# First batches' inverse root on ScalarE, and another order of the first loads, in a resampler-attention and top-1-MoE kernel

## The chip, the cores and the metric

The kernel runs on one core of one Trainium2 chip. The metric is the device time of one execution in microseconds; lower is better. A core has TensorE (PE, with its weight loads as PEld), VectorE (DVE), ScalarE (ACT), GpSimd (POOL) and SyncE (SP). SP, ACT and POOL also issue DMAs, and each of these engines works through its own instructions in the order in which the program gives them.

## The reference, cut to what matters

Sixteen batches of 128 rows of 256 numbers pass through cross-attention and then through a mixture of experts. Everything that the change touches lies in the attention's input side:

```python
def layer_norm(x, w, b):
    mu = jnp.mean(x, axis=-1, keepdims=True)
    var = jnp.var(x, axis=-1, keepdims=True)
    return (x - mu) * jax.lax.rsqrt(var + EPS) * w + b
...
x = layer_norm(x, ln1_w, ln1_b)                        # x here: the context rows
lat = layer_norm(latents, ln2_w, ln2_b)                # latents: _layernorm of the residual rows
lat = lat * (1.0 + scale[:, None, :]) + shift[:, None, :]
q = jnp.einsum('bld,ed->ble', lat, Wq)
kv_in = jnp.concatenate((x, lat), axis=-2)
kv = jnp.einsum('bld,ed->ble', kv_in, Wkv)
k, v = jnp.split(kv, 2, axis=-1)
...
w = jax.nn.softmax(logits.astype(jnp.float32), axis=-1)
out = jnp.einsum('bhqk,bhkd->bhqd', w, v)
```

After the output product the result is added to the residual, normed again, routed to one of eight experts per row and also sent through a shared expert. There are 16 heads of 64; all numbers are float32.

## The kernel before, in words

The batches go in pairs. For a pair `g`, `inputs(g)` or `norms(...)` computes mean and variance of each row, an inverse root of the variance, the normed rows, their transpose, and a scaled and shifted copy `kvT` (columns: 128 context rows and 128 latent rows of a batch). `k_unit(b, j)`, `v_unit(b, j)` and `q_unit(g, j)` are pieces of the products with the weights `wk`, `wv`, `wq`: each fills one PSUM buffer of the pool `ps_m` (three buffers, taken in turn), and ScalarE copies it out (lines 454, 472, 438). `step(u, ...)` handles half the heads of one batch: `logits`, row maxima on DVE, exponents on ScalarE, the division by the sums on POOL, a transpose of the weights through DRAM, and the product with `v`. Between these parts it calls the pieces in the list `units`, in the order of the list, so that PE has work. After the last step come the shared expert, the routing and the experts.

The order on every engine is the order of the calls in the Python code (line 76, `manual_schedule`, for all five engines). Only the data waits are added, and one wait of another sort: each DMA from SP or ACT counts its landing on one of eight counters, and a DMA that takes a counter for the second time waits, on its issuing engine, until the earlier DMA of that counter has landed.

The first pair is handled apart, by `first_inputs(0)` and `first_inputs(1)`, one batch each:

- Lines 97 to 100: DVE clears a tile, and PE runs `WARM` = 9 products on it, so that it isn't idle while the first data travel.
- Lines 281 to 294: the first loads. SP issues `xres` (residual rows of batch 0), `wk` (1024 KB), `xres` of batch 1, the router, and two rows of zeros for DRAM tables; ACT issues `ctx` (context rows of batch 0), `vec` (20 KB: condition vectors and the norms' weights), `ctx` of batch 1, `wv`, `wq` and `wo` (1024 KB each). Of these `wq` waits for the landing of the first `ctx`, `wo` for that of `vec`, and the row of zeros of line 294 for that of `wk`.
- `modulation()` (lines 300 to 310) makes `mod_w` and `mod_b` from `vec` on POOL.
- `first_inputs(i)` (lines 387 to 420): `bn_stats` and `bn_aggr` of the two row tiles (395, 396), the variances (398, 399), then `newton` (line 120): a start value from the bits of the number and three iterations, twelve DVE instructions on 128x2 numbers (lines 124 to 135). `normed` (line 140) makes `fz`, one instruction of 128x256 for each of the two tiles. PE transposes the four 128x128 blocks (410). DVE copies chunk 0 of both tiles into `kvT` (416), ScalarE copies chunk 1 of both (418).
- The calls then are: `modulation`, `first_inputs(0)`, four `k_unit(0, j)`, `first_inputs(1)`, loads of pair 1, `v_unit(0, 0)`, the norms of pair 1, four `q_unit(0, j)`, and `step(0)` with units `k1[0], k1[1], second_inputs, k1[2], k1[3], q[0], q[1]`. `second_inputs` transposes both chunks of pair 1 (359, 360) and loads pair 2.

Outside the first pair, the inverse roots keep `newton` in both kernels.

## Time and profile before

| what | value |
|---|---|
| median of 3 runs | 748.63 us (748.04 to 748.77) |
| the profiled execution's own time | 748.45 us |
| its span, first to last instruction | 746.6 us |
| TensorE clock granted, mean over the span | 0.999 |
| PE busy | 736.0 us (99%) |
| DVE, ACT, POOL busy | 385.8, 259.1, 314.4 us |
| first product with `wk` starts | 9.32 us from the span's start |
| DMA traffic in 0 to 30 us | 5.56 MB |

"Busy" is the time in which an engine has at least one instruction of the program under way. In the timeline a row gives start, duration, engine, source line, operation, what it writes and reads, and in brackets how long the engine had been idle before and what ended that. ACTq and SPq are the sequencers of ACT and SP, where DMAs are issued and where an issue waits. A product of float32 numbers shows as two records, so the nine warm-up products are 18 matmuls.

### The profile page before, as it was taken

Reading aid. Unit: us, or ns where it says so; the run is one execution under the profiler, and the core shown is the slowest. Engines: PE = TensorE matmul, PEld = TensorE weight load, DVE = VectorE, ACT = ScalarE, POOL = GpSimd, SP = SyncE. Lnnn points to the kernel's source line nnn. Section 1 sums busy time; section 2 is a strip of 40 time slices with the busy share of each in tenths; the row PEclk is TensorE's granted clock in tenths of the full one; section 3 lists DMA queues with packets and bytes.
Section 4 is the critical chain, followed back from the end, with each engine's and each line's share of the span. In section 5 each row is a group of like instructions: output and inputs, shape, how many; then the busy total and the mean of one; then the engine's idle time right before and its main releaser. Section 6 shows DMA issues by size and latency. Waiting matters only on the chain.

```text
span 746.6 us, 11560 instructions
## 1 busy us (share of the span) xinstructions
PE 736.0 (99%) x4096; PEld 572.5 (77%) x4096; DVE 385.8 (52%) x949; ACT 259.1 (35%) x787; POOL 314.4 (42%) x366
## 2 busy tenths in 40 slices
PE   8999999999999999999999999999999999999997
PEld 6857768777677677687686788688888877778886
DVE  5566558558647656665656437634643333333321
ACT  2444534444354354344444554611311011111111
POOL 1363554464355445534643654440104334444220
PEclk9999999999999999999999999999999999999999
DMA  8075735844953953864664634651991345645301
GB/s 297 17 250 195 204 128 179 235 165 154 270 170 127 264 200 129 218 223 143 193 197 137 203 124 165 208 183 56 306 322 55 83 110 154 173 138 162 97 27 46
DMA packets 140773, 125.20 MB, mean 168 GB/s; under 512 B 62484, under 2 KB 124631, under 8 KB 140708
## 3 DMA queue, kind: packets, MB, share of 16 engines
q1 hardware_dynamic: 134356, 108.49, 46.8%
q0 software_dynamic: 4336, 12.46, 5.4%
q10 hardware_dynamic: 2016, 3.43, 1.3%
q8 instruction: 35, 0.57, 0.3%
q14 instruction: 30, 0.25, 0.1%
HBM read 75.49 MB, written 49.02 MB: 167 GB/s over the span
## 4 chain that ended last, share of the span: by engine, by line
PE 93%; DVE 4%; ACT 2%; issue 0%; DMA 0%; ACTq 0%
PE pk L446 15%; PE pv L465 14%; PE u_w L1249 11%; PE S L498 8%; PE O L563 8%; PE p L162 8%; PE pw L579 7%; PE pq L431 7%; PE yr L1279 7%; PE ys L192 5%; ACT pe L517 1%; PE pr L634 1%; PE pr L162 1%; PE ys L245 1%; PE slots L983 0%
## 5 line engine op out<-in xcount | busy, mean ns | idle before, releaser
L530 POOL TENSOR_SCALAR pe<-pe,rs 128x256 f32<-128x256 f32 x256 | 232.5, 926 | 243.7 <-DVE rs L527 243.7
L517 ACT ACTIVATE pe<-S,nmx 128x256 f32<-128x256 f32 x256 | 118.7, 489 | 132.0 <-DVE nmx L510 132.0
L465 PE MATMUL pv<-wv,kvT 128*128 128x512 f32 x256 | 116.5, 599 | 0.2 <-ACT kT L454 0.2
L446 PE MATMUL pk<-kvT,wk 128*128 128x256 f32 x512 | 115.2, 383 | 1.3 <-ACT kT L454 0.7
L446 PEld LDWEIGHTS pk<-kvT,wk 128*128 128x128 f32 x512 | 95.8, 190 | 19.4 <-DVE px L539 2.0
L539 DVE STREAM_TRANSPOSE px<-pe 128x512 f32<-128x512 f32 x128 | 81.4, 682 | 32.0 <-POOL pe L530 32.0
L465 PEld LDWEIGHTS pv<-wv,kvT 128*128 128x128 f32 x256 | 47.2, 190 | 53.2 <-issue 50.6
L1249 PE MATMUL u_w<-xT,w 128*128 128x256 f32 (+2 forms) x352 | 85.6, 399 | 0.3
L1249 PEld LDWEIGHTS u_w<-xT,w 128*128 128x128 f32 x352 | 66.0, 190 | 18.8 <-DVE mid_w L1258 3.3
L510 DVE TENSOR_REDUCE nmx<-S 128x4 f32<-128x1024 f32 x64 | 75.1, 1213 | 9.7 <-PE S L498 9.5
L162 PE MATMUL p<-hT,ws 128*128 128x256 f32 x320 | 73.8, 382 | 0.2 <-DVE mid L178 0.2
L162 PEld LDWEIGHTS p<-hT,ws 128*128 128x128 f32 x320 | 59.9, 190 | 10.0 <-issue 1.3
L563 PEld LDWEIGHTS O<-pT,v 128*64 128x64 f32 x1024 | 55.2, 137 | 14.7 <-issue 12.9
L498 PE MATMUL S<-kT,qT 64*128 64x256 f32 x512 | 63.9, 389 | 0.0
L563 PE MATMUL O<-pT,v 128*64 128x128 f32 x1024 | 63.0, 276 | 0.0
L472 ACT COPY v<-pv 128x512 f32<-128x512 f32 x64 | 38.2, 599 | 63.1 <-PE pv L465 63.1
L527 DVE RECIPROCAL rs<-sums 128x4 f32<-128x4 f32 x64 | 11.4, 177 | 93.4 <-ACT pe L517 93.4
L579 PEld LDWEIGHTS pw<-wo,oT 128*128 128x128 f32 x256 | 48.6, 190 | 12.2 <-issue 3.1
L579 PE MATMUL pw<-wo,oT 128*128 128x256 f32 x256 | 57.9, 379 | 0.0
L431 PE MATMUL pq<-kvT,wq 128*128 128x256 f32 x256 | 57.7, 379 | 0.0
L1257 ACT ACTIVATE rsl_w<-u_w 128x256 f32<-128x256 f32 (+2 forms) x40 | 16.0, 400 | 118.8 <-PE u_w L1249 118.8
L517 ACT ACTIVATION_READ_ACCUMULATOR pe<-S,nmx 128x1 f32 x256 | 56.6, 221 | 0.0
(212 smaller groups left out, 748.5 us busy)
## 6 DMA issues: line engine op xcount, KB each, us to landing
p_blocks<-px SPq DMA_DIRECT2D x64, 512.0 KB, 3.2
pT<-p_blocks SPq DMA_DIRECT2D x64, 512.0 KB, 4.2
w<-in_w_dram SPq DMA_DIRECT2D x8, 704.0 KB, 6.3
wds<-in_w_dram SPq DMA_DIRECT2D x8, 640.0 KB, 8.3
w<-in_w_dram SPq DMA_DIRECT2D x8, 640.0 KB, 5.6
t_blocks<-tx SPq DMA_DIRECT2D x12, 256.0 KB, 2.4
kvT<-t_blocks SPq DMA_DIRECT2D x12, 256.0 KB, 6.2
h_rows<-h SPq DMA_DIRECT2D x8, 256.0 KB, 3.1
```

Source lines behind the costliest of these rows:

```text
L162: nc.tensor.matmul(ps, lhsT=shared["w13"][:, c, ds(col, P)], rhs=hT[:, c, ts(t, TB)], start=(c == 0), stop=(c == DC - 1),)
L431: nc.tensor.matmul(pq[:, jj], lhsT=wq[:, c, ts(2 * j + jj, P)], rhs=kvTs[g][:, c, :, 1, :], start=(c == 0), stop=(c == DC - 1),)
L446: nc.tensor.matmul(pk[:, jj, :], lhsT=wk[:, c, ts(2 * j + jj, P)], rhs=kvTs[b // 2][:, c, b % 2].rearrange("p t s -> p (t s)"), start=(c = ...
L465: nc.tensor.matmul(pv, lhsT=kvTs[b // 2][:, c, b % 2, t, :], rhs=wv[:, c, ts(n, 512)], start=(c == 0), stop=(c == DC - 1),)
L498: nc.tensor.matmul(pl[:, r, j, :], lhsT=qTs[b // 2][rows, k, b % 2, :], rhs=kTs[b][rows, k, :], start=True, stop=True,)
L510: nc.vector.tensor_reduce(nmx, pl, AX.X, ALU.max, negate=True)
L517: nc.scalar.activation(pes[u][:, h, :], pl[:, r, j, :], AF.Exp, bias=nmx[:, r, j : j + 1], accum_out=sums[u][:, h : h + 1],)
L530: nc.gpsimd.tensor_scalar(w, w, rs[:, i : i + 1], None, ALU.mult)
L539: nc.vector.transpose(px[:, :, t].rearrange("p j h q -> p h j q"), pes[u][:, ts(n, 4), ts(t, S)].rearrange("p h (j k) -> p h j k", k=BL),)
L563: nc.tensor.matmul(o[r * HD : (r + 1) * HD, j, :], lhsT=vs[b][:, t, ts(2 * (4 * half + j) + r, HD)], rhs=pTs[u][:, j // 2, :, t, 2 * (j % ...
L579: nc.tensor.matmul(pw, lhsT=outT[2 * b + k // 4][:, k % 4, :], rhs=wo[:, k, :], start=(k == 0), stop=(k == NP - 1))
L1249: nc.tensor.matmul(ps[:, k, 0:n], lhsT=w13[:, c, ds(col, P)], rhs=xT[:, c, 0:n], start=(c == 0), stop=(c == DC - 1),)
```

## The change

It touches the warm-up, the loads and the first pair of the attention part, and the list of `step(0)`:

1. `WARM` goes from 9 to 6.
2. `vec` is loaded by SP, right after the first `xres`, no longer by ACT. `wk` becomes two tiles of 512 KB, each with its own DMA on SP, and `k_unit` takes the half that it needs.
3. Router, `wo` and the two rows of zeros are issued by SP in `later_loads()`, called after `first_inputs(0)`; `wo` was on ACT.
4. ACT gets a tiny `Sqrt` at the start, after its second `ctx` load and ahead of `wv` and `wq`; with it comes a table load.
5. In `first_inputs` the twelve instructions of `newton` become a `Sqrt` of 128x2 on ScalarE, and on DVE a multiplication by -0.5, a reciprocal and one Newton step of three instructions.
6. `normed` goes by halves of 128 columns; the two chunks' copies are split by tile (DVE the context's, ScalarE the latents') where they were split by chunk.
7. `step(0)` gets the tiny `Exp` (its table load with it) that the last steps have already, and the two chunks of pair 1's transposes stand in `units` after the first and after the second piece of `k1`.

```diff
-WARM = 9
+WARM = 6
...
-        wk = wts.tile([P, DC, INNER], F32, name="wk")
+        wks = [wts.tile([P, DC, INNER // 2], F32, name=f"wk_{k}") for k in range(2)]
...
         nc.sync.dma_start(out=xres[0][:, 0, :], in_=x[0])
         nc.scalar.dma_start(out=tokens[0][:, 0, :], in_=lat_ctx[0])
-        nc.scalar.dma_start(out=vec, in_=vecs)
-        nc.sync.dma_start(out=wk, in_=wkv_t[:, 0:INNER].rearrange("(c p) e -> p c e", p=P))
+        nc.sync.dma_start(out=vec, in_=vecs)
         nc.scalar.dma_start(out=tokens[0][:, 1, :], in_=lat_ctx[1])
+
+        nc.scalar.activation(spare[0:1, 1:2], spare[0:1, 0:1], AF.Sqrt)
+        for k in range(2):
+            nc.sync.dma_start(
+                out=wks[k],
+                in_=wkv_t[:, ts(k, INNER // 2)].rearrange("(c p) e -> p c e", p=P),
+            )
         nc.sync.dma_start(out=xres[0][:, 1, :], in_=x[1])
         nc.scalar.dma_start(
             out=wv, in_=wkv_t[:, INNER : 2 * INNER].rearrange("(c p) e -> p c e", p=P)
         )
         nc.scalar.dma_start(out=wq, in_=wq_t.rearrange("(c p) e -> p c e", p=P))
-        nc.sync.dma_start(out=wr, in_=router.rearrange("(c p) e -> p c e", p=P))
-        nc.scalar.dma_start(out=wo, in_=wo_t.rearrange("(k p) d -> p k d", p=P))
-        nc.sync.dma_start(out=h_rows[NT : NT + 1, :], in_=zero[0:1, :])
-        nc.sync.dma_start(out=s_rows[NT : NT + 1, :], in_=zero[0:1, :])
+
+        def later_loads():
+            nc.sync.dma_start(out=wr, in_=router.rearrange("(c p) e -> p c e", p=P))
+            nc.sync.dma_start(out=wo, in_=wo_t.rearrange("(k p) d -> p k d", p=P))
+            nc.sync.dma_start(out=h_rows[NT : NT + 1, :], in_=zero[0:1, :])
+            nc.sync.dma_start(out=s_rows[NT : NT + 1, :], in_=zero[0:1, :])
...
-            for r in newton(small, v, 2, "j2"):
-                pass
+
+            root = small.tile([P, 2], F32, tag="froot", name=f"froot_{i}")
+            nc.scalar.activation(root, v, AF.Sqrt)
+            half = small.tile([P, 2], F32, tag="fhalf", name=f"fhalf_{i}")
+            nc.vector.tensor_scalar(half, v, -0.5, None, ALU.mult)
+            y = small.tile([P, 2], F32, tag="fy", name=f"fy_{i}")
+            nc.vector.reciprocal(y, root)
+            a = small.tile([P, 2], F32, tag="fa", name=f"fa_{i}")
+            nc.vector.tensor_tensor(a, y, y, ALU.mult)
+            nc.vector.tensor_tensor(a, a, half, ALU.mult)
+            r = small.tile([P, 2], F32, tag="fr", name=f"fr_{i}")
+            nc.vector.scalar_tensor_tensor(r, a, 1.5, y, ALU.add, ALU.mult)
             z = work.tile([P, 2, D], F32, tag="z", name=f"fz_{i}", bufs=1)
-            for k, t in enumerate(pair):
-                normed(z[:, k, :], t, (mv[:, k, 0:1], r[:, k : k + 1]))
+            for c in range(DC):
+                for k, t in enumerate(pair):
+                    normed(z[:, k, ts(c, P)], t[:, ts(c, P)], (mv[:, k, 0:1], r[:, k : k + 1]))
             for c in range(DC):
                 pt = ps_m.tile([P, 2, S], F32, tag="mm", name=f"fkvt_{i}_{c}")
                 for k in range(2):
                     nc.tensor.transpose(pt[:, k, :], z[:, k, ts(c, P)], ident)
-                for k, (w, o) in enumerate(
...
+                nc.vector.tensor_scalar(
+                    kvTs[0][:, c, i, 0, :],
+                    pt[:, 0, :],
...
+                nc.scalar.activation(
+                    kvTs[0][:, c, i, 1, :],
+                    pt[:, 1, :],
...
-                        lhsT=wk[:, c, ts(2 * j + jj, P)],
+                        lhsT=wks[j // 2][:, c, ts((2 * j + jj) % 4, P)],
...
-            if u // 2 >= B - 2:
+            if u == 0 or u // 2 >= B - 2:
...
         first_inputs(0)
+        later_loads()
...
-        def second_inputs():
-            transpose(range(DC))
-            load_tokens(2)
+        def second_inputs(c):
+            transpose([c])
+            if c == DC - 1:
+                load_tokens(2)
...
-                step(0, k1[:2] + [second_inputs] + k1[2:] + q[:2], [])
+                turns = [lambda c=c: second_inputs(c) for c in range(DC)]
+                step(0, k1[:1] + turns[:1] + k1[1:2] + turns[1:] + k1[2:] + q[:2], [])
```

More of the change, by code (lines that the diff above doesn't have):

```diff
@@ L410, in first_inputs @@
                     nc.tensor.transpose(pt[:, k, :], z[:, k, ts(c, P)], ident)
-                for k, (w, o) in enumerate(
-                    ((vec[:, c, C_W1 : C_W1 + 1], vec[:, c, C_B1 : C_B1 + 1]),
-                     (mod_w[:, c, i : i + 1], mod_b[:, c, i : i + 1]))
-                ):
-                    if c == 0:
-                        nc.vector.tensor_scalar(kvTs[0][:, c, i, k, :], pt[:, k, :], w, o, ALU.mult, ALU.add)
-                    else:
-                        nc.scalar.activation(
-                            kvTs[0][:, c, i, k, :], pt[:, k, :], AF.Identity, bias=o, scale=w
-                        )
+                nc.vector.tensor_scalar(
+                    kvTs[0][:, c, i, 0, :],
+                    pt[:, 0, :],
+                    vec[:, c, C_W1 : C_W1 + 1],
+                    vec[:, c, C_B1 : C_B1 + 1],
+                    ALU.mult,
+                    ALU.add,
+                )
+                nc.scalar.activation(
+                    kvTs[0][:, c, i, 1, :],
+                    pt[:, 1, :],
+                    AF.Identity,
+                    bias=mod_b[:, c, i : i + 1],
+                    scale=mod_w[:, c, i : i + 1],
+                )
         QK = 1.0 / (HD ** 0.5)
```

## The prediction

> **What bounds the kernel now.** I read the page first, its busy shares and the chain that ended last:

> ```profile
> PE 736.0 (99%) x4096; PEld 572.5 (77%) x4096; DVE 385.8 (52%) x949; ACT 259.1 (35%) x787; POOL 314.4 (42%) x366
> ...
> PE 93%; DVE 4%; ACT 2%; issue 0%; DMA 0%; ACTq 0%
> ```

> PE is full almost all of the span, so a change elsewhere counts only by the time for which PE stands still. The view of waits, for PE alone, says where it does (total, times, longest):

> ```profile
> PE pk L446 <- ACT kT L454: 0.7, 1, 0.7
> PE pk L446 <- DVE kvT L416: 0.7, 1, 0.7
> PE fkvt L410 <- DVE fz L140: 0.6, 1, 0.6
> ...
> PE pv L465 <- ACT kT L454: 0.2, 1, 0.2
> ```

> Three belong to the start, one (ACT kT, at 33 us) to step 0. The warm-up products before the first transposes, 1.27 to 7.32, are empty too: what counts is when K of batch 0 begins. From there PE has next to no gap until 475 us, so a shift of K reaches the end in full. The timeline of the start:

> ```profile
> 3.69 0.43 DVE L395 BATCH_NORM_STATS2 fst<-ctx 128x6 f32<-128x256 f32 x1 [2.48 <-DMA ctx<-in_lat_ctx_dram]
> ...
> 5.09 0.17 DVE L124 TENSOR_SCALAR j2h<-fv 128x2 f32<-128x2 f32 x1
> ...
> 7.33 0.41 DVE L140 TENSOR_SCALAR fz<-ctx,fmv,j2y 128x256 f32<-128x256 f32 x1
> 7.33 0.38 ACTq L292 DMA_DIRECT2D wo<-in_wo_t_dram  x1
> ...
> 7.74 1.28 ACT L418 ACT_TABLE_LOAD   x1 [7.74 <-DMA vec<-in_vecs_dram]
> ...
> 8.42 0.23 SPq L294 DMA_DIRECT2D s_rows<-zero  x1
> ...
> 9.32 7.31 PE L446 MATMUL pk<-kvT,wk 128*128 128x256 f32 x32 [0.65 <-DVE kvT L416]
> ```

> Statistics from 3.69, root from 5.09 to 7.33, K at 9.32. Line 292, `wo`, waits on ACT for the landing of `vec` at 7.3, and ACT's table load, which waits for nothing itself, starts only after that issue: an issue that waits holds all of ScalarE's work behind it. Line 294 waits for `wk`, so `wk` landed at 8.4. The windows show what the DMA engines moved then (last column GB/s):

> ```profile
> 5.00:6.00 1.00, 1.00 (x6) 0.88 (x5) 0.83 (x7) 0.00 (x0) 0.00 (x0) 1.00 0.86 247
> 6.00:7.00 1.00, 1.00 (x7) 0.82 (x5) 0.83 (x6) 0.00 (x0) 0.00 (x0) 1.00 0.93 265
> 7.00:8.00 1.00, 0.44 (x3) 0.14 (x1) 0.93 (x4) 0.26 (x1) 0.58 (x2) 1.00 0.96 347
> 8.00:9.00 1.00, 0.67 (x4) 0.31 (x3) 0.57 (x3) 1.00 (x1) 0.92 (x4) 1.00 1.07 404
> ```

> With 18, 227, 329 and 302 before, 876 KB had moved by 5.0.

> [...] The DMA view of 7.5 to 8 agrees: 59 packets of ACT's queue (0.14 MB) beside 61 of SP's (0.05 MB), equal in number, not in bytes. [...] The trace has the 1.28 but no drain: work starts at 9.04, 0.02 after the load. [...] The trace agrees: warm-up products start 0.43 us apart until 5.2 and 0.22 after; and PE's last product ends at 741.2, where the windows of the tail (first column after the comma PE, clock third from the end) show the clock full until 745 and falling after:

> ```profile
> 741.00:745.00 4.00, 0.18 (x1) 0.00 (x0) 0.42 (x1) 0.00 (x0) 0.00 (x0) 1.00 0.14 41
> 745.00:746.60 1.60, 0.00 (x0) 0.00 (x0) 0.00 (x0) 0.00 (x0) 0.00 (x0) 0.77 0.02 5
> ```

> **The change, part by part.**

> *ScalarE's queue, first batch.* The changed program, built, gives ACT: two `ctx` issues, table load, tiny root, `wv` (waits for `vec`), `wq` (waits for the second half of `wk`, whose counter it takes over), and only then the root of batch 0. So the root is not ready at 5.1, but when that half has landed. When is that? Ahead of it on SP stand `xres`, `vec` (20 KB) and the first half; with both `ctx` that is 3x131+20+524 = 938 KB, moved at about 5.25. `vec` follows `xres`, which landed by 3.57 (line 293 waits for it): about 4.1. So `wv` is issued at 4.1, and flows from about 5.3 (the first issue at 0.82 shows traffic about 1.1 us later), just when the second half starts. Halves have 2 KB packets, `wv` 4 KB: taken in turn, 524 KB of `wk` go with 1049 of `wv`; 1573 KB at the rates above end near 9.9, landing 0.5 later: 10.4. Shared by bytes (1049 KB) it is 9.1; with `wv` behind it, 7.7. The small `vec` packets that disturbed 4 to 7 us are gone, so I take 9.6; ends 7.7 and 11.

> Then: issue of `wq` 0.41 (as `wo`), root at 10.0. Root 0.22 (a 128x16 ACT row), reciprocal 0.18 (L527), three short DVE steps at the 0.20 pitch of `newton`, with waits: halves of `fz` at root+1.05 and +1.25 (a 128x256 takes 0.41; 0.28 estimated for half), transposes done at +1.95 (0.43 from `fz`'s end to copy, as at 8.06 to 8.49), DVE's copy 0.41. ScalarE's copy of the chunk is built to wait for DVE's, not beside it: 0.46 more. K at root+2.95 = 12.95. Before 9.32: **+3.65**. Without the hold the root would run at 5.1 and K at 8.1: -1.3.

> *Second batch.* Before, `fz` of batch 1 was done at 13.57, and PE went from K (ends 16.63) into its transposes and to V at 17.31, 0.68 later. Now the root of batch 1 stands on ACT behind the four copies `kT`, the last of which can start only when K ends:

> ```profile
> 16.67 0.58 ACT L454 COPY kT<-pk 128x512 f32<-128x512 f32 x1 [1.14 <-PE pk L446]
> ...
> 17.31 1.98 PE L465 MATMUL pv<-wv,kvT 128*128 128x512 f32 x4 [0.24 <-ACT kT L454]
> ```

> Root at K's end +0.53 (ACT's next starts 0.49 after a copy), transposes from +1.9 to +2.6, V at +2.75: **+2.1**. PE has nothing else before them in its order. Q, 1.8 after V, finds `kvT` ready.

> *Step 0.* The `Exp` table load and tiny act (1.28+0.20) lie in ACT's idle 1.74 before the exponents at 28.57: 0, at most 1.5 uncovered. The chunk apart lets the third `pk` take a buffer that DVE empties, not the one behind the exponents: the 0.68 at 33 goes, **-0.7** (0 if another wait takes it).

> *Clock.* Six warm-up products end near 6.0 (9 records of 0.43, the rest 0.22). PE is then idle until the transposes at 11.4: 5.4 us, against 4.7 from the last product to the drop at the end of the trace. So the clock likely drops and K starts at half speed, for a total of about 3.9 us of work as at the start (1.27 to 5.16). Transposes at 11.4 mean full speed at about 15.3; 2.35 us of K at half speed lose **+1.2**; ends 0 and 2.3 (all of 4.6).

> *Loads moved for nothing.* `wo` on SP at 3.7 is behind both halves; it is needed at step 3. `wq` at 9.6 instead of 3.7 is needed near 24 and the same 5.2 MB ended at 18.6 before: covered by 5 us. `ctx` of pair 1 waits for `fz` of batch 1, now near 22 instead of 13.2: landing about 25, its norms 5.1 us on DVE (18.6 to 23.75 before), 30; first needed by the row maxima near 33: covered by 3.

> Sum 3.65+2.1-0.7+1.2 = +6.25. The profiled execution's 748.45 is its span 746.6 and 1.85 around it; it lies 0.18 below the median of the runs. 748.45+6.25 = **754.7**.

> **Rivals.** (1) As forecast, but the clock stays: 753.5. For it: the idle is near the limit. (2) The second half of `wk` lands at 7.7, `wv` behind it: root 8.1, K 11.05, +1.75+2.1-0.7, the idle under 4 us: 751.6. Against it: equal packet counts. (3) The counter's wait ends before 5: K at 8.1, -1.3+2.1-0.7: 748.5, no change. It needs 1 MB in 3 us. (4) Faster: neither root is held by what stands ahead of it on ScalarE; -1.3 and -0.7, no second stall: 746.4. It decides if the first root runs by 5.3 and the second within 0.5 us of its variances. Against it is the table load at 7.74.

> **Numbers.** Forecast 0.46, (1) 0.22, (2) 0.14, (3) 0.10, (4) 0.08. A difference under 0.2% (1.5 us) can't be told from none. Slower 0.46+0.22+0.14 = 0.82, same 0.10, faster 0.08. The range leaves out (3) and (4): from 751.0, just under (2), to 757.0 (second half at 11, clock at 2.3, less half of both, since they seldom meet).

> **What would show it.** Right: `wq`'s issue on ACT near 9.6 and `froot` behind it; K near 13; `fkvt` of batch 1 waiting 2 us on `fz`; no wait of `pk` on `kT` in step 0; K's first records at twice 0.22 us. Wrong: `froot` at 5.2, or V within 1 us of K's end.

## The result and the profile after

Over six runs each on the same chip, the changed kernel took 757.76 us (median; 754.41 to 758.18) and the kernel before 748.70 (748.04 to 751.01). The medians are 9.1 us apart; the ratio over all runs is 1.0109, 95% interval 1.0095 to 1.0124 (the medians alone make 1.0121). The forecast was 754.7, 6.25 slower than the profiled execution before. The profiled execution took 757.67, its span is 755.9 and the clock granted to TensorE, averaged over the span, 0.989; before 748.45, 746.6 and 0.999.

The page after, busy shares and the chain that ended last:

```profile
PE 739.7 (98%) x4090; PEld 574.5 (76%) x4090; DVE 384.8 (51%) x939; ACT 261.8 (35%) x792; POOL 314.2 (42%) x366
...
PE 93%; DVE 3%; ACT 1%; DMA 1%; issue 0%; SPq 0%; ACTq 0%
```

The new entry is a DMA: `wk` now stands in the chain with 1%. PE has six records fewer, the three warm-up products, and yet is busy for 3.7 us more, so part of the loss is products that run slower. The stalls of PE, times in which it waits for data, are the other part (total, times, longest):

```profile
PE fkvt L429 <- DVE fz L140: 7.2, 2, 5.2
...
PE pk L470 <- ACT kvT L438: 0.6, 1, 0.6
```

Before, `fkvt` waited once, for 0.6. Now both batches wait for their normed rows, 5.2 and 2.0 us. The wait of `pk` on `kT` at 33 us is gone. The timeline of the start, with the rows that answer to those of before:

```profile
3.71 0.46 ACTq L293 DMA_DIRECT2D wv<-in_wkv_t_dram  x1
...
4.90 0.17 DVE L414 TENSOR_SCALAR fhalf<-fv 128x2 f32<-128x2 f32 x1
...
9.34 0.38 ACTq L296 DMA_DIRECT2D wq<-in_wq_t_dram  x1
...
9.77 0.20 ACT L412 ACTIVATE froot<-fv 128x2 f32<-128x2 f32 x1 [6.53 <-DMA wk<-in_wkv_t_dram]
...
10.79 0.35 DVE L140 TENSOR_SCALAR fz<-ctx,fmv,fr 128x128 f32<-128x128 f32 x1
...
13.01 10.11 PE L470 MATMUL pk<-kvT,wk 128*128 128x256 f32 x32 [0.57 <-ACT kvT L438]
...
23.15 0.59 ACT L478 COPY kT<-pk 128x512 f32<-128x512 f32 x1 [1.14 <-PE pk L470]
...
23.64 0.21 ACT L412 ACTIVATE froot<-fv 128x2 f32<-128x2 f32 x1
...
25.16 1.15 PE L429 MATMUL fkvt<-ident,fz 128*128 128x128 f32 x4 [2.04 <-DVE fz L140]
...
26.10 3.44 PE L489 MATMUL pv<-wv,kvT 128*128 128x512 f32 x4
...
29.37 7.07 PE L455 MATMUL pq<-kvT,wq 128*128 128x256 f32 x32
...
36.37 2.00 PE L522 MATMUL S<-kT,qT 64*128 64x256 f32 x16
...
49.74 2.00 PE L522 MATMUL S<-kT,qT 64*128 64x256 f32 x16
```

The first root's input is ready when line 414 runs, at 4.90. The root itself runs at 9.77, and its bracket says why: ScalarE had been idle for 6.53 us, and what ended that was the landing of `wk`. Between the two lies the issue of `wq` at 9.34. The second root, at 23.64, stands directly behind the last copy `kT`. K of batch 0 has the same 32 records as before and takes 10.1 us instead of 7.3; V's four records take 3.44 instead of 1.98.

The last two rows are the first scores, the products of `qT` with `kT`, of step 0 and of the step after it. Before, those stood at 26.13 and 40.44 (the second row ends with its view, two records early):

```profile
26.13 2.00 PE L498 MATMUL S<-kT,qT 64*128 64x256 f32 x16
...
40.44 1.78 PE L498 MATMUL S<-kT,qT 64*128 64x256 f32 x14
```

Set side by side, the two profiled executions account for the whole difference:

| stretch | before | after | difference |
|---|---|---|---|
| start to K of batch 0 | 9.32 | 13.01 | +3.69 |
| K itself | 7.31 | 10.11 | +2.80 |
| K's end to V | 0.68 | 2.98 | +2.30 |
| V to Q | 1.82 | 3.27 | +1.45 |
| first scores of step 0 to the next scores | 14.31 | 13.37 | -0.94 |
| sum | | | +9.30 |

The spans differ by 9.3 and the times by 9.22, so nothing of size is left for what comes after the second scores.

The second and fourth rows are the clock. PE alone in windows of 3.413 us (the clock in the trace changes at 8.744, 18.984, 25.810 and 29.224, so its stretches are 3, 2 and 1 times this); after the comma PE's busy time, then the granted clock:

```profile
5.33:8.74 3.41, 0.79 (x4) 1.00 0.87 261
8.74:12.16 3.41, 0.87 (x4) 0.50 1.03 396
12.16:15.57 3.41, 2.85 (x8) 0.50 1.06 390
15.57:18.98 3.41, 3.41 (x9) 0.50 0.44 161
18.98:22.40 3.41, 3.41 (x17) 1.00 0.00 0
22.40:25.81 3.41, 1.35 (x7) 1.00 0.00 0
25.81:29.22 3.41, 3.41 (x6) 0.50 0.48 154
```

In these rows each window's clock goes with what PE did in the one before. After 0.79 us of work it is halved; it comes back only after a window that is full, 15.57 to 18.98, so K runs 5.97 us at half speed. After the window with the second stall, 1.35 us of work, it is halved again for one window, and that is where V lies.

### The profile page after: what moved, and what is told of

It reads as the page before. It is cut to its first block, busy times and chain, and to the rows that moved or that the text cites. A ratio compares the mean times of both kernels' runs of the same rounds, so it can differ in the third digit from the quotient of the medians.

```text
span 755.9 us, 11545 instructions
## 1 busy us (share of the span) xinstructions
PE 739.7 (98%) x4090; PEld 574.5 (76%) x4090; DVE 384.8 (51%) x939; ACT 261.8 (35%) x792; POOL 314.2 (42%) x366
## 3 DMA queue, kind: packets, MB, share of 16 engines
q10 hardware_dynamic: 832, 2.36, 0.8%
## 4 chain that ended last, share of the span: by engine, by line
PE 93%; DVE 3%; ACT 1%; DMA 1%; issue 0%; SPq 0%; ACTq 0%
PE pk L470 15%; PE pv L489 14%; PE u_w L1276 11%; PE S L522 8%; PE O L587 8%; PE p L162 8%; PE pw L603 7%; PE pq L455 7%; PE yr L1306 7%; PE ys L192 5%; DMA wk<-in_wkv_t_dram 1%; PE pr L658 1%; PE pr L162 1%; PE ys L245 1%; ACT pe L541 0%; PE slots L1010 0%
## 5 line engine op out<-in xcount | busy, mean ns | idle before, releaser
L470 PE MATMUL pk<-kvT,wk 128*128 128x256 f32 x512 | 118.0, 389 | 0.6 <-ACT kvT L438 0.6
L470 PEld LDWEIGHTS pk<-kvT,wk 128*128 128x128 f32 x512 | 97.9, 194 | 19.0 <-DVE px L563 2.0
L551 DVE RECIPROCAL rs<-sums 128x4 f32<-128x4 f32 x64 | 11.4, 178 | 92.6 <-ACT pe L541 92.6
(215 smaller groups left out, 748.7 us busy)
```

Of the source, the lines that this page charges most:

```text
L470: nc.tensor.matmul(pk[:, jj, :], lhsT=wks[j // 2][:, c, ts((2 * j + jj) % 4, P)], rhs=kvTs[b // 2][:, c, b % 2].rearrange("p t s -> p (t s)"),
```

## The experiments

The leading theory after the result: two stalls, each of a root that stands on ScalarE behind something that it doesn't need, and each with a loss of clock behind it. The rivals: the DMA traffic at the start delays K whatever ScalarE does; the new arithmetic itself is slower; the shorter warm-up is the cause.

**One part of the hold taken away: e1_no_hold.** `wq` is issued by SP, so no issue that waits stands ahead of the first root.

```diff
-        nc.scalar.dma_start(out=wq, in_=wq_t.rearrange("(c p) e -> p c e", p=P))
...
         def later_loads():
+            nc.sync.dma_start(out=wq, in_=wq_t.rearrange("(c p) e -> p c e", p=P))
```

> The changed kernel with the load of wq issued by SP in later_loads, so that nothing on ScalarE waits for the second half of wk. If the hold on ScalarE made the first stall: root of batch 0 near 5.0 instead of 9.77, K near 8.0 instead of 13.01, no gap of 5 us and no half clock in K; the second stall (2.04 before the transposes of batch 1) stays. Time 748.5, or up to 1.7 more where the clock still drops after the second stall. If the new root with its halves and copies is what costs, K stays near 13 and the time near 757.7.

Measured: 750.07 us (20 runs), 1.0014 [1.0006, 1.0023]; the profiled execution 748.32. Its timeline:

```profile
4.91 0.20 ACT L412 ACTIVATE froot<-fv 128x2 f32<-128x2 f32 x1 [1.67 <-DVE fv L407]
...
8.22 7.17 PE L470 MATMUL pk<-kvT,wk 128*128 128x256 f32 x32 [0.78 <-ACT kvT L438]
...
17.43 1.01 PE L429 MATMUL fkvt<-ident,fz 128*128 128x128 f32 x4 [2.04 <-DVE fz L140]
```

The root runs as soon as its variances are there, K begins at 8.22 and takes 7.17, and the second stall is there as before, 2.04. From the changed kernel this is -4.79 for K's start and -2.94 for its length, 7.73 together; the medians differ by 7.69. So one issue of 0.38 us, by where it stands, costs 7.7 us. Five of the 20 runs lie at 748.3 to 748.6, fourteen of the other fifteen between 749.7 and 751.2, and one at 754.16. In the profiled one, of the lower group, PE worked 1.57 us in the window of the second stall and the clock stayed:

```profile
13.82:17.23 3.41, 1.57 (x8) 1.00 0.91 298
17.23:20.64 3.41, 3.19 (x11) 1.00 0.55 177
```

The others' mean clock is mostly 0.996 against 0.998, so that they lost the window after the stall is likely, but no trace of one of them shows it.

**The second root alone: e2_second_newton.** Batch 1 keeps the steps on DVE, batch 0 the root on ScalarE.

```diff
+            if i == 1:
+                for r in newton(small, v, 2, "j2"):
+                    pass
+            else:
+                root = small.tile([P, 2], F32, tag="froot", name=f"froot_{i}")
...
```

> The changed kernel with newton on DVE for batch 1 alone; batch 0 keeps ScalarE's root. If the second stall comes from the root's place behind the four kT copies: the 2.04 us gap before the transposes of batch 1 goes, and with it the clock's second drop (about 1.7): 757.7 - 3.7 = 754.0, K still at 13.0. If PE waits there for a PSUM buffer that the copies empty, the gap stays and the time is 757.

Measured: 754.58 us (4 runs), 1.0074 [1.0059, 1.0088]. Between K and V there is no wait on `fz` any more, and the clock is half only once, from about 9.0 to 19.3 (its mean is 0.54, 0.50, 0.50 and 0.96 in the four windows from 8.74 to 22.40, and 1.00 in the next two):

```profile
10.55 0.20 ACT L416 ACTIVATE froot<-fv 128x2 f32<-128x2 f32 x1 [7.32 <-DMA wk<-in_wkv_t_dram]
...
13.79 9.87 PE L474 MATMUL pk<-kvT,wk 128*128 128x256 f32 x32 [0.57 <-ACT kvT L442]
...
24.34 1.98 PE L493 MATMUL pv<-wv,kvT 128*128 128x512 f32 x4 [0.24 <-ACT kT L482]
```

From the changed kernel that is -3.2, in the medians and in the traces: 2.30 less between K and V, 1.45 less between V and Q, where the half-speed window had been, and 0.24 less in K, but a K that began 0.78 later, since the first root ran at 10.55. The expectation, 754.0, didn't have this later start.

**Both: e3_both.** The edits of e1 and e2 together.

> Both edits: wq on SP, and newton for batch 1. If the two places on ScalarE are the whole loss, what is left of the change is a gain: K at 8.0 (-1.3), step 0 without its 0.68: 748.5 - 2.0 = 746.5. If the changed loads or the halves cost something of their own, it is 748 or more.

Measured: 746.79 us (10 runs), 0.9975 [0.9965, 0.9984]. The first edit is worth 7.7 alone and 7.8 beside the second; the second 3.2 and 3.3. They add up, and with both the kernel is faster than before. The rest of the change, taken together, doesn't cost: it gains. The new arithmetic isn't the cause, nor the traffic at the start as such. Six warm-up products don't cost anything here either; whether nine would have spared some of the clock while the first root is held was not tried. K begins 1.0 earlier than before, and V waits for `wv`, which the stall had hidden:

```profile
8.31 7.22 PE L474 MATMUL pk<-kvT,wk 128*128 128x256 f32 x32 [0.57 <-ACT kvT L442]
...
16.38 1.96 PE L493 MATMUL pv<-wv,kvT 128*128 128x512 f32 x4 [0.41 <-DMA wv<-in_wkv_t_dram]
```

**The clock alone: e4_warm18 and e9_filled.** Both stalls stay; what PE does in them changes. In e4 the warm-up fills the first (`WARM = 18`); in e9 four products without use also lie in the second:

```diff
-WARM = 6
+WARM = 18
...
+                if i == 1 and c == 0:
+                    fill = ps_o.tile([P, NP // 2, S], F32, tag="O", name="fill")
+                    for _ in range(4):
+                        nc.tensor.matmul(fill[:, 0:2, :]..., lhsT=idle[:, 0, 0:P], rhs=idle[:, 0, :], ...)
```

> The changed kernel with 18 warm-up products instead of 6, which keep PE busy from 1.27 to about 11.1, just short of the transposes at 11.29. No data and no wait is changed. If K's first half ran at half clock because PE had been idle: K still starts at 13.0, takes 7.3 instead of 10.1 us, and the time is 757.7 - 3.0 = 754.7. If the idle time has nothing to do with the clock, 757.7.

> The changed kernel with 18 warm-up products and four more idle products (1.7 us at full clock) in the place where PE waits 2.04 us for the transposes of batch 1. Both stalls of the data stay, K starts at 13.0, V 2.75 after K's end; only the clock can differ. If the second half-clock stretch costs 1.7 us and comes from that stall's idle time, every run lies near 752.7, the lowest of the kernel with 18 warm-up products, and the clock stays full. If it has another cause, the times are spread from 752.7 to 755.2 as there.

Measured: e4 754.35 us (4 runs), 1.0063 [1.0046, 1.0081]; e9 753.34 (4 runs, 753.12 to 753.91), 1.0068 [1.0052, 1.0085] of the runs of before beside it, whose median was 748.39. PE of e4, then PE of e9:

```profile
13.21 7.18 PE L470 MATMUL pk<-kvT,wk 128*128 128x256 f32 x32 [0.61 <-ACT kvT L438]
22.44 1.01 PE L429 MATMUL fkvt<-ident,fz 128*128 128x128 f32 x4 [2.04 <-DVE fz L140]
23.28 3.23 PE L489 MATMUL pv<-wv,kvT 128*128 128x512 f32 x4
```

```profile
13.07 7.25 PE L480 MATMUL pk<-kvT,wk 128*128 128x256 f32 x32 [0.55 <-ACT kvT L448]
20.16 1.89 PE L430 MATMUL fill<-idle 128*128 128x256 f32 x8
22.36 1.00 PE L439 MATMUL fkvt<-ident,fz 128*128 128x128 f32 x4 [0.31 <-DVE fz L140]
23.20 1.89 PE L499 MATMUL pv<-wv,kvT 128*128 128x512 f32 x4
```

K starts 0.1 to 0.2 later than in the changed kernel, and takes 7.2: the first loss of clock is worth 2.9 in K. The medians say 3.4, but two of e4's four runs, at 752.71 and 753.63 with clock 0.998, seem not to have had the second loss. In the profiled one, at 755.17, V still takes 3.23, and the window before it shows the clock's reason again:

```profile
20.27:23.69 3.41, 1.35 (x6) 1.00 0.00 0
23.69:27.10 3.41, 3.41 (x6) 0.50 0.48 158
```

With the fill V takes 1.89 in the same place. It is the traces that show this second loss: the stretch from V to Q is 3.03 in e4 and 1.73 in e9, 1.3 less. The times don't settle it, since the two ratios, 1.0063 and 1.0068, are the same within their intervals and e4's runs are of both sorts. e9's runs lie 0.6 above the 752.7 that was expected, but within 0.8 us of each other, as was expected if nothing but the clock spreads them. With its clock full (1.00 from 5 to 30 us), e9 is still about 5 us slower than the kernel before beside it. That is what the waits themselves cost: 3.69 and 2.30 less step 0's 0.94 make 5.05.

**The list of step 0 alone: e5_split_only.** The kernel before, with only the two chunks of pair 1's transposes put apart.

```diff
-                step(0, k1[:2] + [second_inputs] + k1[2:] + q[:2], [])
+                step(0, k1[:1] + turns[:1] + k1[1:2] + turns[1:] + k1[2:] + q[:2], [])
```

> The kernel before with one part of the change alone: the two chunks' transposes of pair 1 apart in the units of step 0. Expected: the 0.68 us in which PE waits for a kT copy near 33 us goes, nothing else moves, 748.7 - 0.7 = 748.0. If the wait only changes its place, 748.7 with another gap of PE in step 0.

Measured: 747.95 us (20 runs), 0.9990 [0.9983, 0.9996]. The scores of step 0 and of the next step stand 13.37 us apart, as in the changed kernel, against 14.31:

```profile
26.65 2.00 PE L498 MATMUL S<-kT,qT 64*128 64x256 f32 x16
...
40.02 2.00 PE L498 MATMUL S<-kT,qT 64*128 64x256 f32 x16
```

This part is a gain of 0.8 by the medians, so small that 20 runs were needed to tell it from none.

**What the root is worth: e6_newton_all.** The kernel e3 with the steps on DVE for both batches (`if i < 2`), and `WARM = 9`.

> The kernel with both edits (wq on SP, newton for batch 1), but newton for batch 0 as well and 9 warm-up products: no root on ScalarE is left. It says what the root itself is worth where nothing holds it. The root path takes about 1.0 us from the variances to the halves of fz, newton 2.2: K about 1.2 us later than 8.31, time 746.8 + 1.2 = 748.0. If K waits for the weights or the vectors and not for the root, 746.8 as with the root.

Measured: 747.93 us (12 runs), 0.9989 [0.9981, 0.9998]. K begins at 9.58, with the root at 8.31: the replaced steps are worth 1.27 in K's start and 1.14 in the medians.

**The copies: e7_chunks.** The kernel e3 with the copies divided by chunk as before, so that ScalarE doesn't wait for DVE's copy out of the same tile (in e3's trace its first copy, at 7.78, ends an idle time of 2.36 that is put down to DVE's `kvT`).

```diff
-                nc.vector.tensor_scalar(kvTs[0][:, c, i, 0, :], pt[:, 0, :], ...)
-                nc.scalar.activation(kvTs[0][:, c, i, 1, :], pt[:, 1, :], ...)
+                for k, (w, o) in enumerate(...):
+                    if c == 0:
+                        nc.vector.tensor_scalar(kvTs[0][:, c, i, k, :], pt[:, k, :], w, o, ALU.mult, ALU.add)
+                    else:
+                        nc.scalar.activation(kvTs[0][:, c, i, k, :], pt[:, k, :], AF.Identity, bias=o, scale=w)
```

> The kernel with both edits and the copies split by chunk again, as in the kernel before (DVE chunk 0, ScalarE chunk 1). In the change ScalarE's copy of a chunk waits for DVE's of the same chunk. Expected: that wait goes, the last copy ends about 0.3 us earlier, 746.8 - 0.3 = 746.5, hardly to be told from 746.8 by the time, but by the start of K and the copies in the trace. If the two engines run side by side in the change, nothing moves.

Measured: 746.27 us (6 runs), 0.9964 [0.9952, 0.9976], the lowest median of all. Its timeline at the copies:

```profile
7.64 0.40 DVE L439 TENSOR_SCALAR kvT<-fkvt,mod_w,mod_b 128x128 f32<-128x128 f32 x1
7.83 0.46 ACT L441 ACTIVATE kvT<-fkvt,vec 128x128 f32<-128x128 f32 x1 [2.36 <-PE fkvt L433]
8.18 0.45 ACT L441 ACTIVATE kvT<-fkvt,mod_b,mod_w 128x128 f32<-128x128 f32 x1
8.32 0.89 PE L469 MATMUL pk<-kvT,wk 128*128 128x256 f32 x3 [0.54 <-DMA wk<-in_wkv_t_dram]
```

ScalarE's copies begin when PE's transposes are done and overlap with DVE's. K begins no earlier (8.32, against 8.31), because now it waits for the first half of `wk`: one wait has taken another's place. That the median is 0.5 below e3's isn't explained by K's start; in the profiles V waits 0.15 less, and the intervals of the two overlap.

**`wq` behind the root on the same queue: e8_wq_behind_root.** The kernel e7, with `wq` issued by ScalarE again, but in `later_loads()`, which comes after the root of batch 0.

```diff
-            nc.sync.dma_start(out=wq, in_=wq_t.rearrange("(c p) e -> p c e", p=P))
+            nc.scalar.dma_start(out=wq, in_=wq_t.rearrange("(c p) e -> p c e", p=P))
```

> As the chunk kernel, but wq is issued by ScalarE again, behind the root and the copies of batch 0, where it still waits for the second half of wk. If only what stands behind that issue matters, the hold costs nothing there: the first kT copy is due near 10, when that half has landed. wv no longer shares the DMA engines with wq, so V's wait for wv (0.41 in the kernel with both edits) goes: about 746.2. If the wait itself costs wherever it stands, 2 us more than that.

Measured: 746.42 us (6 runs), 0.9969 [0.9957, 0.9981]. The same issue on the same engine, with the same wait for the second half of `wk`:

```profile
10.06 0.38 ACTq L298 DMA_DIRECT2D wq<-in_wq_t_dram  x1
10.48 0.59 ACT L477 COPY kT<-pk 128x512 f32<-128x512 f32 x1 [1.88 <-PE pk L469]
...
18.49 7.14 PE L454 MATMUL pq<-kvT,wq 128*128 128x256 f32 x32 [0.43 <-DMA wq<-in_wq_t_dram]
```

It leaves at 10.06. The copy behind it comes 2.36 us after K's start, where in e7 it came after 2.00, so the hold is there, about 0.4 us, but PE has no wait from it. V's wait for `wv` is gone, but Q waits 0.43 for `wq`, so nothing is won over e7. The median is 0.15 above e7's, well within the intervals. With e1 this shows that neither ScalarE as issuer nor the wait as such is the harm, only what is queued behind it.

## Why the prediction was right, and where it was off

*The time as a whole* came at the edge. The range ended at 757.0. The ratio of 1.0109, on the 748.45 that the forecast started from, makes 756.6, just inside; the median, 757.76, and the profiled execution, 757.67, lie above. And 757.0 doesn't follow from the terms given for it: 1.4 for a second half at 11 and 1.1 for a clock loss of 2.3, less half of both, end at about 756. The direction and the two stalls were forecast; what they took from the clock was not, in its size.

*The first root held.* Right in its mechanism: +3.65 forecast, +3.69 measured; `wq` issued at 9.34 (9.6), root at 9.77 (10.0), K at 13.01 (12.95). That the size fits so closely is partly luck: the root came 0.23 early, and the way from the root to K took 3.24 where 2.95 was forecast. e1 shows the cause.

*How the landing of `wk` was reached* was wrong; that its number held was luck. The step said that `wv` flows from about 5.3 and takes its turns, packet by packet, with the second half. The DMA view of 5 to 7 us shows one queue, SP's:

```profile
DMA packets 277, 0.50 MB, mean 252 GB/s; under 512 B 19, under 2 KB 43, under 8 KB 277
...
q1 hardware_dynamic: 277, 0.50, 79.9%
```

ACT's queue has no line there: it moved nothing. `wv`, issued at 3.71, had its first packets at about 7.85, and only 30 of them by 9. So until then the equal packet counts that the step carried over from the kernel before (59 beside 61 from 7.5 to 8) had nothing to apply to: only one of the two queues moved packets. Nor did the rate rise without the small packets of `vec`, which the step held to blame for the rate of 4 to 7 us before: from 4 to 8 it was 229, 238, 266 and 240 GB/s, where it was 302, 247, 265 and 347 before. This doesn't clear those packets, since `wk`'s own packets had also gone from 4 to 2 KB. The step took the right time from too much traffic at too high a rate. Why `wv` began so late is open; no run tried it.

*The second root.* Right: +2.1 forecast, +2.30 measured, with the root 0.53 after K's end, as said, and the stall 2.04. e2 shows it.

*The clock* is the term that was mis-sized: +1.2 forecast, +2.80 in K and +1.45 between V and Q measured, 4.25 together. The forecast had the clock drop near 11 and return at 15.3, after 3.9 us of work counted from the transposes at 11.4. It dropped at 8.74 and returned at 18.98. Its range for the first loss (0 to 2.3) ended below what came. Two things failed: the work was counted from PE's first instruction, not in whole windows, so the window to 15.57 with 2.85 us of work, which didn't bring the full clock back, was counted as if it did; and only the long idle time was asked about, not the stall of 2.04 that the same text forecast between K and V. A window in which PE was busy for 1.35 of 3.41 us, 40%, was enough there for the next to be at half clock.

*Step 0*: -0.7 forecast, -0.94 measured in the changed kernel and in e5. *Covered for nothing*: all held. The table load and tiny `Exp` end at 38.59, and the exponents at 38.81 wait for the row maxima; `wq` landed at about 17.8 and is needed at 29.37; the norms of pair 1 ended at 33.5, before the row maxima at 37.56.

*The rivals.* (1), the clock stays, is what e9 makes by hand; forecast 753.5, measured 753.34. (3), the first root free, is e1: forecast 748.5, profiled 748.32, median 750.07 with the second loss of clock that it left out. (4), neither root held, is close to e3, where batch 1 has no root on ScalarE: forecast 746.4, measured 746.79. (2) had `wv` wait behind all of `wk`, which is nearly what it did, but the second half landed at about 9.3 and not at 7.7. So the waits in the sum were right in four combinations, and what it lacked was the clock behind a stall.

## What to carry to other kernels

Before an operation is moved to an engine that also issues DMAs, list what stands ahead of it on that engine and what each of these waits for, counter reuse among it: here an issue of 0.38 us in the wrong place cost 7.7 us, and 0 behind the root. The same holds for work behind a copy that waits for PE: a step that is shorter by itself (1.1 us for batch 0 in e6) lost 2 when it stood at the end of such a row, for batch 1. And a stall of PE is priced with its clock: here one of 2.04 us, with work on both sides, cost 1.45 more in the changed kernel and nothing more in e1's profiled run.

## What was not expected of the hardware

The windows don't lie alike: full clock begins at 5.161 in one of the two traces and at 5.330 in the other, with PE's first product at 1.27 in both. That a stall of 2 us falls differently on them in each run is the author's estimate; it would explain why the same program varies: 754.41 to 758.18 with mean clocks of 0.994 to 0.989 in the changed kernel, two groups about 1.7 us apart in e1, and 0.8 us in all in e9, all four runs of which have clock 0.998. It is not the only thing that varies: three of e5's 20 runs, without such a stall, lie about 2 us above the others with clock 0.996, and one trace of each kernel doesn't show why.

In the changed kernel `wv`, a DMA of 4 KB packets issued on ACT's queue at 3.71, had its first packet at 7.85, 4.1 us later, though that queue moved nothing between while SP's was busy (652 packets of SP's queue from 3.5 to 7.85, none of ACT's). Before, `wv` was issued at 2.25 and had its first packet at 6.79, but there `vec` and `ctx` were still moving on the same queue.
